# One of a band's sixteen transfers moves from SyncE's queue to GpSimd's

## The chip, the cores and the metric

The kernel runs on one core of a Trainium2 chip. The core has a matrix engine (TensorE, called PE in the profile), three engines for elementwise work (VectorE or DVE, ScalarE or ACT, GpSimd or POOL) and SyncE (SP), which here does nothing but issue DMA transfers. GpSimd issues transfers too. The transfers of both run on the same 16 DMA engines. Each engine works through its own list of instructions in order, and they wait for each other by semaphores. The metric is the time of one execution on the device in microseconds.

## What is computed

The input is `x`, 32 images of 256 channels and 32 x 32 pixels in float32. Two layers are added to it in turn:

```python
    # --- layer 0 (conv_preact) ---
    x = x + _L0_conv_ref(_gn(x), L0_conv_weight, L0_conv_bias)
    # --- layer 1 (conv_preact) ---
    x = x + _L1_conv_ref(_gn(x), L1_conv_w1, L1_conv_bn_gamma, L1_conv_bn_beta, L1_conv_bn_mean, L1_conv_bn_var, L1_conv_w2, L1_conv_b2)
```

`_gn` is a group norm with 32 groups. Layer 0 is a 3 x 3 convolution from 256 to 256 channels with its operands and its result rounded to a 16-bit float. Layer 1 is an involution: every pixel computes its own 7 x 7 filter for each of 16 groups of channels, and that filter is applied to the normalised input around the pixel:

```python
        y = jnp.einsum('oc,bchw->bohw', w1, x)
        ...
        w = jnp.einsum('oc,bchw->bohw', w2, y) + b2[None, :, None, None]
        w = w.reshape(b, G, K * K, H, W)
        ...
        out = jnp.einsum('bgkhw,bgckhw->bgchw', w, patches)
```

## The kernel before

An image passes through two halves that overlap with those of its neighbours. The front half (`front`) does the norm, the 3 x 3 convolution (line 332), the second norm and the transposed pixels (line 396). The back half is the involution, and it has a detour through memory in the middle.

`weights` (line 411, PE) computes the filters of four image rows at a time, and `evict` (line 435, DVE) adds their bias and lays them into the ring buffer `w_sb` in SBUF. `scatter` (line 476, SP) writes the filters of eight image rows into the scratch tensor `wd` in device memory, in seven transfers of 160 KB, so that each pixel's filter lands at a shifted place. `load_bands` (line 497) reads the same eight rows back as a band: a matrix that says how every source pixel of these rows contributes to the pixels in its 7 x 7 surroundings. `sums` (line 522, PE) multiplies pixels by the band in 128 small matmuls per band, and `add_windows` (line 538, DVE) adds the result into `x`. `store` (line 543, SP) writes the image out, and `load_x` (line 106, SP) brings in later images.

There are four bands to an image and so 128 in all. A band is read in 16 transfers, one for each value of `j`, which is a column of a half image. Most are of 70.5 KB; the three columns nearest the image's edge have part of their filter cut off and are shorter: `j` = 0 has 40.5 KB, `j` = 1 has 50.5 KB and `j` = 2 has 60.5 KB. The transfers are issued in the order of the list `ORDER`, and the list `BY_SYNC` names the values of `j` that SP issues:

```python
BY_SYNC = (0, 1)
ORDER = (0, 4, 8, 2, 12, 5, 9, 13, 3, 1, 6, 10, 14, 7, 11, 15)
...
            queue = nc.sync if j in BY_SYNC else nc.gpsimd
```

So POOL issues 14 of a band's 16 transfers and SP two. POOL does nothing else after the start. SP has the scatters, the images' loads and the stores between its band transfers.

The order of the work is written by hand. A loop counts steps `n`; an image takes 16 of them (`per`), a band four. `sums` of a band stands at its step, `weights` 18 steps ahead (`LEAD`), the scatters one and two steps behind the weights that complete them, and `load_bands` nine steps ahead of the use (`due(n, 3 - 4 * NBAND)`). There are three band buffers (`NBAND`). A band's transfers wait until PE has finished with the band three before it, and until the scatter of their rows has landed. The transfers of each queue take eight completion semaphores in turn. An issue on POOL waits for the landing of the transfer that was issued eight before it on POOL; SP has eight semaphores of its own.

Of the kernel before, what the change touches and what calls it, by code (L numbers as in the profile page):

```python
# [62 lines left out]
ROW = S * WPIX  # L63
WR = 4
NBAND = 3
BY_SYNC = (0, 1)
ORDER = (0, 4, 8, 2, 12, 5, 9, 13, 3, 1, 6, 10, 14, 7, 11, 15)
NPIX = 6
RING = 32
# [9 lines left out]
def tile_quant_conv_then_involution(  # L79
# [398 lines left out]
    def load_bands(b, k):  # L478
# [3 lines left out]
        for i, j in enumerate(ORDER):  # L482
# [12 lines left out]
            )  # L495
            queue = nc.sync if j in BY_SYNC else nc.gpsimd
            queue.dma_start(to, src)  # L497
# [140 lines left out]
```

## Time and profile before

| what | value |
|---|---|
| runs, median (lowest to highest) | 1353.61 us (1353.46 to 1360.37) |
| the profiled execution's own time | 1351.29 us |
| its span, first to last instruction | 1349.5 us |
| PE busy | 1247.6 us, 92% |
| POOL busy | 1012.5 us, 75% |
| DVE, ACT busy | 827.1 us, 734.2 us |
| moved by DMA | 361.85 MB, 268 GB/s over the span |
| band issues on POOL, line 497 | 1792, mean 550 ns, median 548 |
| band issues on SP, line 497 | 256, median 593 ns |

The profile is one execution. An issue of a transfer counts as busy time on POOL, but not on SP, whose issues appear only in the timeline and in the rows of a single line. A wait is put down to what ended last before the engine went on: "POOL band L497 <- DMA band<-wd" is time in which POOL stood before an issue of line 497 until a transfer from `wd` into a band had landed. "issue" as the cause means that the profile shows none. The three numbers of a wait are its total in us, how often it occurred, and the longest. A row of a group gives busy time, mean ns of one instruction, and the idle time of the engine just before them with what ended most of it. The chain that ended last is followed back from the last instruction, at each step to what released it.

### The profile page before, as it was taken

To read this page: it belongs to the slowest core of one execution; us is meant where nothing else is said; L and a number is where in the kernel's file an instruction comes from. 1 tells how busy PE (TensorE), PEld (TensorE's weight loads), DVE (VectorE), ACT (ScalarE), POOL (GpSimd) and SP (SyncE) were. 2 spreads that over 40 slices of the span, in tenths; PEclk is the share of its full clock that TensorE was granted. 3 is DMA by queue.
4 is the path that set the end of the run, shared out by engine and by line. 5 is a ranking of instruction groups with operands and counts; after the bars stand their busy time and mean duration, and the time that the engine had idled before them with its cause. 6 is when DMAs were issued, how large, how long until landed. Compare 5 with 4: busy or idle time off the path is not lost.

```text
span 1349.5 us, 65799 instructions
## 1 busy us (share of the span) xinstructions
PE 1247.6 (92%) x27648; PEld 757.6 (56%) x27648; DVE 827.1 (61%) x2539; ACT 734.2 (54%) x1731; POOL 1012.5 (75%) x1818
## 2 busy tenths in 40 slices
PE   4899999999989999999999999999999999999664
PEld 2355556655545665555566556555655556555453
DVE  5456656666656666666666566666666566566542
ACT  5875655555646556565555556555656565563300
POOL 9067777787778778877778777777877877788885
PEclk9999999999999999999999999999999999999997
DMA  6089999999999999999999999999999999999995
GB/s 227 6 236 295 270 271 284 283 278 296 282 271 286 297 287 281 298 282 281 267 285 287 260 282 282 271 284 284 288 285 278 274 280 278 277 285 262 282 270 157
DMA packets 360724, 361.85 MB, mean 268 GB/s; under 512 B 75056, under 2 KB 304752, under 8 KB 359152
## 3 DMA queue, kind: packets, MB, share of 16 engines
q1 hardware_dynamic: 278512, 229.38, 56.5%
q0 software_dynamic: 81920, 128.28, 33.5%
q8 instruction: 220, 3.60, 1.1%
q14 instruction: 72, 0.59, 0.1%
HBM read 176.60 MB, written 180.76 MB: 265 GB/s over the span
## 4 chain that ended last, share of the span: by engine, by line
PE 58%; DMA 24%; POOL 8%; issue 4%; DVE 3%; ACT 2%; SPq 1%; POOLq 0%; DVEq 0%; ACTq 0%
PE pc L332 24%; DMA band<-wd 19%; PE acc L522 18%; PE pw L411 10%; POOL band L497 8%; DMA wd<-w_sb 4%; PE py L377 3%; PE pt L396 3%; ACT junk L214 1%; DVE w_sb L435 1%; SPq L476 1%; DVE wq L195 1%; DVE x L538 1%; DMA band<-in_w 1%; DMA out<-x 0%
## 5 line engine op out<-in xcount | busy, mean ns | idle before, releaser
L497 POOL DMA_DIRECT2D band<-wd x1792 | 980.8, 550 | 320.5 <-DMA band<-wd 189.9
L435 DVE TENSOR_TENSOR w_sb<-pw,late_sb 128x224 f32<-128x224 f32 (+7 forms) x1280 | 331.4, 324 | 423.6 <-PE pw L411 423.4
L332 PE MATMUL pc<-xq,wq 128*128 128x496 f16 (+3 forms) x2304 | 535.1, 378 | 25.0 <-ACT xq L273 20.6
L522 PE MATMUL acc<-band,pixels 64*32 64x190 f32 (+1 forms) x16384 | 423.5, 330 | 55.5 <-DMA band<-wd 44.2
L522 PEld LDWEIGHTS acc<-band,pixels 64*32 64x32 f32 x16384 | 301.6, 107 | 164.7 <-issue 88.9
L332 PEld LDWEIGHTS <-wq 128*128 128x128 f16 x2304 | 206.3, 98 | 322.9 <-issue 106.7
L411 PE MATMUL pw<-late_sb,y 64*32 64x224 f32 (+1 forms) x8192 | 285.0, 330 | 14.1 <-issue 12.7
L538 DVE TENSOR_TENSOR x<-acc,x 128x380 f32<-128x380 f32 (+1 forms) x512 | 262.4, 513 | 35.5 <-PE acc L522 26.6
L411 PEld LDWEIGHTS pw<-late_sb,y 64*32 64x32 f32 x8192 | 183.7, 105 | 38.7 <-issue 22.3
L400 ACT COPY pixels<-pt 128x512 f32<-128x512 f32 x128 | 73.8, 577 | 226.5 <-PE pt L396 226.5
L214 ACT ACTIVATE junk<-x 128x512 f16<-128x512 f32 (+1 forms) x192 | 146.4, 762 | 11.9 <-DVE x L348 9.4
L214 ACT ACTIVATE junk<-x,mean 128x1024 f16<-128x1024 f32 x128 | 147.1, 1149 | 4.3
L245 ACT ACTIVATE s<-back,eps 128x2 f32<-128x2 f32 x64 | 18.9, 296 | 178.8 <-DVE back L230 178.8
L273 ACT ACTIVATE xn<-x,off,rstd 128x512 f32<-128x512 f32 x128 | 96.1, 800 | 0.0
L346 DVE TENSOR_SCALAR q<-pc 128x512 f16<-128x512 f32 x128 | 87.2, 681 | 13.3 <-PE pc L332 13.3
L348 DVE SCALAR_TENSOR_TENSOR x<-q,early_sb,x 128x512 f32<-128x512 f16 x128 | 94.7, 740 | 0.3
L396 PE MATMUL pt<-ident,xn 128*128 128x128 f32 x512 | 77.8, 275 | 1.5 <-ACT pixels L400 1.4
L396 PEld LDWEIGHTS pt<-ident,xn 128*128 128x128 f32 x512 | 63.7, 142 | 27.3 <-issue 2.8
L273 ACT ACTIVATE xq<-x,off,rstd 128x1024 f16<-128x1024 f32 x64 | 75.6, 1227 | 0.0
L235 ACT ACTIVATE mean<-back 128x2 f32<-128x2 f32 x64 | 12.6, 196 | 100.0 <-DVE back L230 100.0
L377 PE MATMUL py<-xn,early_sb 128*64 128x512 f32 x256 | 62.2, 605 | 0.9 <-ACT xn L273 0.9
L388 ACT ACTIVATE y<-py,bn_shift,bn_scale 128x256 f32<-128x256 f32 x64 | 32.5, 557 | 23.3 <-PE py L377 23.0
(40 smaller groups left out, 368.2 us busy)
## 6 DMA issues: line engine op xcount, KB each, us to landing
wd<-w_sb SPq DMA_DIRECT2D x896, 160.0 KB
band<-wd POOLq DMA_DIRECT2D x1664, 70.5 KB
x<-in_x SPq DMA_DIRECT2D x64, 512.0 KB
out<-x SPq DMA_DIRECT2D x64, 512.0 KB
band<-wd POOLq DMA_DIRECT2D x128, 60.5 KB
band<-wd SPq DMA_DIRECT2D x128, 50.5 KB
band<-wd SPq DMA_DIRECT2D x128, 40.5 KB
band<-in_w SPq DMA_DIRECT2D x2, 1152.0 KB
```

The lines of the kernel that those rows point to most:

```text
L214: nc.scalar.activation(junk[:, n0:n1], src[:, h, n0:n1], func, bias=bias, accum_out=self.sums[:, i : i + 1])
L273: nc.scalar.activation(dst, src, AF.Identity, bias=self.off[:, one], scale=self.rstd[:, one])
L332: nc.tensor.matmul(pc.rearrange("p (r c) -> p r c", c=W)[:, r0 - nt * RT : r1 - nt * RT, c0:c1], wq[:, kh, k, mh * P : (mh + 1) * P], xq[: ...
L346: nc.vector.tensor_scalar(q, pc, F16_MAX, -F16_MAX, ALU.min, ALU.max)
L348: nc.vector.scalar_tensor_tensor(xt[:, mh, cols], q, bias_sb[:, mh : mh + 1], xt[:, mh, cols], ALU.add, ALU.add)
L377: nc.tensor.matmul(py[i * CR : (i + 1) * CR], w1_sb[:, kh, :], px[:, :, i], start=kh == 0, stop=kh == CH - 1,)
L396: nc.tensor.transpose(pt[:, i, h * P : (h + 1) * P], xn[:, h, (m + i) * P : (m + i + 1) * P], ident)
L411: nc.tensor.matmul(pws[i][t * TW : (t + 1) * TW, : dj.stop - dj.start, r], y_sb[b % 2][half, (r0 // 2 + r) * W : (r0 // 2 + r + 1) * W], w ...
L435: nc.vector.tensor_tensor(to, of[:, :, d0:d1], bias[:, :, d0:d1], ALU.add)
L497: queue.dma_start(to, src)
L522: nc.tensor.matmul(at[t * TW : (t + 1) * TW, h, :, f - top : l - top], px[p, a, v * GC : v * GC + TW], of[:, :, a, f - top : l - top, v], ...
L538: nc.vector.tensor_tensor(x_at, of, x_at, ALU.add)
```

## The change

The transfer with `j` = 1 is issued by GpSimd in place of SyncE. SP keeps `j` = 0 alone, and POOL issues 15 transfers for each band. In POOL's list the transfer comes ninth of fifteen, as `ORDER` says.

```diff
--- before.py
+++ after.py
@@ -63,7 +63,7 @@
 ROW = S * WPIX
 WR = 4
 NBAND = 3
-BY_SYNC = (0, 1)
+BY_SYNC = (0,)
 ORDER = (0, 4, 8, 2, 12, 5, 9, 13, 3, 1, 6, 10, 14, 7, 11, 15)
 NPIX = 6
 RING = 32
```

## The prediction

> **What bounds the kernel now.** I read the page's table of engines first, then the chain that ended last, then the waits of PE and of POOL, then POOL's row among the groups, and last the stretches of POOL alone.
>
> ```profile
> PE 1247.6 (92%) x27648; PEld 757.6 (56%) x27648; DVE 827.1 (61%) x2539; ACT 734.2 (54%) x1731; POOL 1012.5 (75%) x1818
> ...
> PE 58%; DMA 24%; POOL 8%; issue 4%; DVE 3%; ACT 2%; SPq 1%; POOLq 0%; DVEq 0%; ACTq 0%
> ```
>
> By busy time PE is the bound. The chain gives PE 58%, but a third of the span (DMA 24%, POOL 8%) runs over the band loads and the engine that issues them, so PE is not alone.
>
> ```profile
> L497 POOL DMA_DIRECT2D band<-wd x1792 | 980.8, 550 | 320.5 <-DMA band<-wd 189.9
> ```
>
> This is GpSimd's whole steady work: 1792 issues (128 bands of 14), 550 ns each. The reader is to see that its 75% is not idle for want of a task; the waits, POOL's and one of PE's, say what fills the rest:
>
> ```profile
> POOL band L497 <- DMA band<-wd: 189.9, 246, 3.6
> ...
> POOL band L497 <- DMA wd<-w_sb: 62.8, 27, 38.2
> POOL band L497 <- issue: 52.9, 61, 3.7
> PE acc L522 <- DMA band<-wd: 44.2, 19, 5.9
> ...
> POOL band L497 <- PE pt L396: 5.7, 4, 2.0
> ...
> POOL band L497 <- PE acc L522: 0.7, 3, 0.4
> ```
>
> A band's first issue has to wait until PE has freed the band buffer. POOL loses only 0.7 us to that in the whole run: the buffer has always been free for a while when POOL comes to it. So POOL is never ahead. What it waits for is its own earlier transfers (189.9 us, 246 times): in the order of instructions with their semaphores POOL's transfers take eight completion semaphores in turn, and each issue waits for the landing of the one eight before it. I call this the lane wait. 38.2 us of the 62.8 us on `wd` is a single wait, at the start. PE in turn waits 44.2 us for bands. POOL's stream of issues and PE run at nearly the same pace, and POOL is the one that is behind.
>
> The pace in stretches of POOL's issues (us, then busy and count, granted clock, DMA share, GB/s):
>
> ```profile
> 400.00:600.00 200.00, 156.90 (x288) 1.00 0.98 289
> ...
> 800.00:1000.00 200.00, 154.47 (x283) 1.00 0.96 283
> 1000.00:1200.00 200.00, 151.37 (x277) 0.99 0.95 278
> 1200.00:1250.00 50.00, 41.31 (x77) 1.00 0.94 273
> ```
>
> An issue comes every 0.69 to 0.72 us, and every 0.65 us once the last images have been loaded. The DMA engines are 94 to 98% busy, so bytes are close to a limit too. POOL's first issue starts at 73.1 us, its last ends at 1336.2 us (the row of line 497): 1263.1 us for 1792, 0.705 us each. 13.3 us remain to the end of the span.
>
> **The time that the sum is made against.** The profiled execution took 1351.3 us, span 1349.5 and 1.8 around it. The median of the runs is 2.3 us higher, which is added at the end.
>
> **The change, part by part.** In each of 128 bands the transfer with j = 1 (50.5 KB) leaves SP's queue for POOL's. PE, DVE and ACT keep their order; bytes, buffers and the shape of the transfer stay.
>
> SP loses 128 of 256 band issues. Their row has a median of 593 ns, so some 76 us of issue time go. I cost this at nothing: SP's queue has 1% of the chain, and it has waits of its own on DVE (150.7 us for `w_sb`) to fall back on. What was queued behind the moved issue, the scatters, can be issued 0.6 us earlier per band, which bears on POOL's wait for `wd` below.
>
> POOL gains 128 issues: 128 x 0.550 = +70.4 us. In the new order the issue stands ninth of fifteen, behind the transfer j = 3, and six further issues of its band are queued behind it. PE waits for the last of these. Nothing hides this: POOL waits for no other engine long enough, and cover would have to come out of its own waits. They are, term by term:
>
> - Lane waits. Now 189.9 / 1792 = 0.106 us per transfer. If that pace holds, 128 more transfers cost 128 x 0.106 = +13.6 us. From the other side: between 1200 and 1250 us, without image loads, the wait is 6.0 us for 77 transfers, 0.078 each; 1920 x 0.078 = 149.8, or -40.1 us. A longer run spreads the same bytes and lightens the DMA engines (283 GB/s now in the middle, a few per cent less then), which shortens landings; but a band's image loads and stores stay. I take the middle, -13.2 us.
> - Waits of no shown cause (52.9 us): 61 of them, spread over the stream, so by count, 52.9 x 128 / 1792 = +3.8 us.
> - Waits for `wd`: 62.8 - 38.2 = 24.6 us can go, as POOL comes later to each band and SP's scatters are issued earlier; or nothing goes, as a slower POOL also holds back PE, DVE and the scatters. Half: -12.3 us.
> - Waits for PE (pt 5.7, acc 0.7, pw 0.7 us): too small to count.
>
> Sum: 70.4 - 13.2 + 3.8 - 12.3 = +48.7 us, or 1400 us on the profiled execution and 1402 us on the median (3.6% up). All of it reaches the end, because POOL's last band is followed only by the 13.3 us tail. As a pace: (1263.1 + 48.7) / 1920 = 0.683 us per transfer. Ends: low 70.4 - 40.1 + 3.8 - 24.6 = +9.5, 1363 us; high 70.4 + 13.6 + 3.8 = +87.8, 1441 us, which is the present pace times fifteen.
>
> A rule weighed against the rows. The two queues' issue costs are 548 ns median for POOL and 593 for SP in the rows of line 497, so the move makes no single issue dearer. The Trainium skill, "DMA: Bandwidth & Descriptors", section "SWDGE vs HWDGE vs iDMA", sends plain copies to SP or ACT because their setup is faster. That speaks against the move but for a reason that this row does not show. The same page, section "Issuing engines are not separate DMA queues", says that spreading issues over engines saves only the time to initiate, usually small beside the transfer. By it the move would be worth almost nothing and the time would stay at 1354. The trace's answer is that initiating is not small here: 981 us of POOL's 1263.
>
> **The rivals.**
>
> A. Hidden: no change, 1351 to 1354 us on the median. PE is 92% busy and waits for bands 44.2 us in only 19 waits; three band buffers could soak up a later POOL. For no change the pace must reach 1263.1 / 1920 = 0.658 us per transfer, which only the 1200 to 1250 stretch beats (0.649). Against it: a stock of ready bands would show as POOL waiting for a free buffer, and that is 0.7 us.
>
> B. The pace does not improve at all, or gets worse: 1441 us and above. For it: the stretches from 400 to 1200 us differ by only 4% in pace whatever the DMA share. Against: the image-free stretch, and a DMA load that must fall as the run grows.
>
> C. Faster, by one mechanism: SP's queue, lighter by one transfer per band, leaves the DMA engines to POOL's transfers, these land before their lane is wanted again, and the lane waits collapse. It decides below the pace of 0.658. The other gaps after the change are (52.9 + 3.8 + 62.8 + 7.1) / 1920 = 0.066 us, so with the 0.550 of an issue the lane wait would have to fall below 0.042 from 0.106. At 0.028 the time would be 1920 x 0.014 = 27 us less, 1327 us. It is bounded by PE's 44.2 us of band waits: not below 1309. Against: the DMA engines move the same bytes, and the lowest lane wait in a stretch is 0.078.
>
> D. That SP's part of a band is what PE waits for, so that the move takes it off the late queue. PE's chain enters bands through POOL's issues (8%) and not SP's (1%, its scatters). If it were so, up to the 44.2 us of PE's waits would be at stake, less what POOL adds. I give it no chance of its own; it is in C.
>
> **How the numbers follow.** The forecast (pace 0.668 to 0.700, 1373 to 1434 us) 0.73; B with its approaches (over 1434) 0.11; a cheap outcome, 1361 to 1373, 0.05; A, within 0.5% (1347 to 1360; 0.5% is about what a measurement here can tell from no change), 0.07; C 0.04. The range runs from the low end of the sum, 1363, to its high end, 1440: about 0.14 lies below and 0.05 above. Faster 0.04, same 0.07, slower 0.89.
>
> **What would show it.** In the profile after: POOL's row at line 497 x1920, still near 550 ns, some 1056 us busy; POOL's share of the span at 78%; POOL's wait for its own bands between 150 and 204 us; still no wait of POOL for acc; PE's wait for bands well above 44 us and PE's share near 89%; the chain moved from PE to DMA and POOL; DMA moving near 258 GB/s over the span. I am wrong if an issue on POOL lasts longer, if lane waits fall below 0.05 us per transfer (A or C), or if PE's band waits don't grow.

## The result, and the profile after

The change makes the kernel slower: median 1427.15 us (1422.48 to 1429.03) against 1353.53 us, a ratio of 1.056 (95% interval 1.0527 to 1.0593), some 74 us. The prediction said 1402 us, between 1363 and 1440.

The profiled execution after took 1427.95 us, 76.7 us more than that of before. Its engines and the chain that ended last, from the page:

```profile
span 1426.2 us, 65827 instructions
...
PE 1275.1 (89%) x27648; PEld 775.9 (54%) x27648; DVE 819.1 (57%) x2539; ACT 736.0 (52%) x1731; POOL 1085.7 (76%) x1946
...
PE 45%; DMA 32%; POOL 8%; issue 5%; DVE 4%; SPq 3%; ACT 3%; POOLq 0%; DVEq 0%; ACTq 0%
```

PE's share of the chain falls from 58% to 45% and DMA's rises from 24% to 32%. PE is busy for 89% of the span, not 92%. The cost stands in POOL's row, and the waits tell how it is made up (total us, times, longest):

```profile
L497 POOL DMA_DIRECT2D band<-wd x1920 | 1051.6, 550 | 326.7 <-DMA band<-wd 194.9
```

```profile
POOL band L497 <- DMA band<-wd: 194.9, 231, 2.8
...
PE acc L522 <- DMA band<-wd: 80.6, 41, 4.9
POOL band L497 <- issue: 57.7, 79, 3.0
POOL band L497 <- DMA wd<-w_sb: 54.5, 35, 36.3
```

The row adds up to the whole rise. Busy time goes from 980.8 to 1051.6 us (+70.8), the idle time before the issues from 320.5 to 326.7 (+6.2): together +77.0, where the span grew by 76.7. That the sum comes out is no proof by itself, since POOL's list runs in both kernels from shortly after the start (first issue at 73.1 and 71.0 us) to 13 us before the end. What the row shows is which part grew: 128 more issues at an unchanged 550 ns took 71 us, and POOL's waits together got no shorter to make room for them (those for `wd` fell from 62.8 to 54.5 us, the others grew by more). PE's wait for bands went from 44.2 to 80.6 us.

The time that SP gained turned into waiting. Its largest waits after (SP's own queue, same columns):

```profile
SPq L476 <- DVE w_sb L435: 355.0, 98, 47.6
SPq L106 <- DMA out<-x: 115.2, 27, 6.3
```

Its wait for the filters in `w_sb` was 150.7 us before and is 355.0 us now: SP stands in front of its scatters until DVE has written the filters. About half of that rise is SP's own freed time, since the same wait is 260.5 us in a kernel below in which SP has one band transfer and the run is as quick as before. That the rest comes from PE waiting longer for bands is argued from the order of the work, not shown.

### The profile page after: what moved, and what is told of

Its sections match the earlier page's. It is cut to its first block, busy times and chain, and to the rows that moved or that the text cites. A ratio compares the mean times of both kernels' runs of the same rounds, so it can differ in the third digit from the quotient of the medians.

```text
span 1426.2 us, 65827 instructions
## 1 busy us (share of the span) xinstructions
PE 1275.1 (89%) x27648; PEld 775.9 (54%) x27648; DVE 819.1 (57%) x2539; ACT 736.0 (52%) x1731; POOL 1085.7 (76%) x1946
## 2 busy tenths in 40 slices
DMA packets 361748, 361.87 MB, mean 254 GB/s; under 512 B 77104, under 2 KB 306800, under 8 KB 360176
## 4 chain that ended last, share of the span: by engine, by line
PE 45%; DMA 32%; POOL 8%; issue 5%; DVE 4%; SPq 3%; ACT 3%; POOLq 0%; DVEq 0%; ACTq 0%
DMA band<-wd 24%; PE pc L332 17%; PE acc L522 15%; PE pw L411 9%; POOL band L497 8%; DMA wd<-w_sb 7%; SPq L476 3%; PE py L377 3%; DVE w_sb L435 2%; PE pt L396 1%; ACT junk L214 1%; DVE x L538 1%; DMA band<-in_w 1%; ACT xn L273 0%; DVE x L348 0%
## 5 line engine op out<-in xcount | busy, mean ns | idle before, releaser
L497 POOL DMA_DIRECT2D band<-wd x1920 | 1051.6, 550 | 326.7 <-DMA band<-wd 194.9
L522 PE MATMUL acc<-band,pixels 64*32 64x190 f32 (+1 forms) x16384 | 438.7, 336 | 102.2 <-DMA band<-wd 80.6
L522 PEld LDWEIGHTS acc<-band,pixels 64*32 64x32 f32 x16384 | 312.3, 108 | 216.3 <-issue 119.1
L411 PE MATMUL pw<-late_sb,y 64*32 64x224 f32 (+1 forms) x8192 | 294.4, 336 | 20.2 <-issue 18.7
L411 PEld LDWEIGHTS pw<-late_sb,y 64*32 64x32 f32 x8192 | 191.0, 107 | 47.2 <-issue 30.5
## 6 DMA issues: line engine op xcount, KB each, us to landing
band<-wd POOLq DMA_DIRECT2D x128, 60.5 KB, 3.9
band<-wd POOLq DMA_DIRECT2D x128, 50.5 KB, 4.9
```

What stands on the lines that cost most here:

```text
L411: nc.tensor.matmul(pws[i][t * TW : (t + 1) * TW, : dj.stop - dj.start, r], y_sb[b % 2][half, (r0 // 2 + r) * W : (r0 // 2 + r + 1) * W], w ...
L522: nc.tensor.matmul(at[t * TW : (t + 1) * TW, h, :, f - top : l - top], px[p, a, v * GC : v * GC + TW], of[:, :, a, f - top : l - top, v], ...
```

## The experiments

Theory: the time is set by POOL's list of issues; one more issue per band costs its 0.55 us and the list's usual waits, whatever it carries. I call it the stream theory. Rivals were that the 50.5 KB on another queue cost the time, that SP's lighter list does, and that PE or the DMA engines bind so that POOL's list matters little. Ratios are against the kernel before, run beside each group of experiments on the same chip.

### One more issue that carries almost nothing

```diff
             queue.dma_start(to, src)
+            if j == 1: nc.gpsimd.dma_start(spare, bass.AP(tensor=src.tensor, offset=src.offset, ap=[src.ap[0], src.ap[1], [1, PAD]]))
```

This is put into the kernel before, with a small tile `spare`.

> SP keeps its two transfers of a band; POOL issues a fifteenth per band, right behind j = 3, that reads 8 floats for each of 16 rows (512 bytes) into a spare tile. Nothing of the result depends on it. Stream theory (the time is set by POOL's list of issues, and an issue costs 0.55 us and its share of the waits whatever it carries): 1415 to 1430 us, as with the moved transfer, POOL's row x1920. Rival (the cost is that 50.5 KB more go through POOL's queue, and landings get later for it): the small one costs little, below 1380 us. Rival (what SP no longer issues makes the rise, through an order that suited less): 1354 us.

Measured: 1421.9 us, ratio 1.0475 (1.0415 to 1.0534). The added issue's line (its duration in ns, lowest, median and highest, and the first and last start) with the time from issue to landing in us, and the two waits:

```profile
L498 POOL DMA_DIRECT2D spare<-wd x128: 567/567/570, 75.4 to 1403.4; - x128
...
DMA to landing us min/median/max: 2.2/5.1/7.8
```

```profile
POOL band L497 <- DMA band<-wd: 167.6, 201, 2.8
...
PE acc L522 <- DMA band<-wd: 68.6, 39, 5.7
```

A transfer of 512 bytes that nobody reads costs 0.0475 x 1357.65 = 64 us, or 0.50 us per issue; the moved 50.5 KB cost 0.056 x 1353.53 = 76 us, 0.59 each. So most of the cost is the place in POOL's list. The difference of about 11 us is for bytes and landings, if it is real: the two intervals just overlap. The added issue also takes its turn among the eight semaphores, so its 0.567 us on POOL and its turn are not told apart here.

### The moved transfer issued by nobody

```diff
-        for i, j in enumerate(ORDER):
+        for i, j in enumerate(j for j in ORDER if j != 1):
```

> The transfer j = 1 is issued by nobody; POOL has 14 and SP one. The part of the result that comes from these columns is left out. It is the change without POOL's part. Stream theory: POOL's list is that of the kernel before, so 1345 to 1355 us; at most some 20 us less if 3% fewer bytes shorten landings (lane waits 189.9 to 170). Rival (an SP that is lighter lets its scatters burst against POOL's transfers): above 1375 us.

Measured: 1355.8 us, ratio 1.001 (0.9976 to 1.0044). Taking the issue from SP is worth nothing that can be told from zero, even with its bytes gone too (355.22 MB moved for 361.85). POOL's wait for its own transfers was not less, and SP's wait for the filters grew:

```profile
POOL band L497 <- DMA band<-wd: 200.6, 247, 2.8
```

```profile
SPq L476 <- DVE w_sb L435: 260.5, 92, 48.0
```

The two halves of the change thus stand apart: SP's half is near 0, and POOL's half is 64 us for the issue alone and about 76 us with the bytes.

### Sixteen and thirteen on POOL

```diff
-BY_SYNC = (0, 1)
+BY_SYNC = ()          # e16
+BY_SYNC = (0, 1, 2)   # e13
```

> SP issues none of a band's transfers, POOL all 16. Stream theory: the pace after was (1413.0 - 71.0) / 1920 = 0.699 us for each; at 2048 the time is 2048 x 0.699 + 85 + 2 = 1518 us, or 90 us over the changed kernel; with nothing but the issue's own 0.55 us it is 70 us over, 1497 us. Rival (DMA engines get free as the run grows, and landings get shorter): below 1475 us. Lane waits near 190 us in total if only the issue is added, 207 us if they go with the count.

> SP issues j = 0, 1 and 2, POOL 13. Stream theory: 1664 x 0.70 = 1165 us for POOL's list alone, 1252 us in all, so POOL is no longer what ends last; PE is, with its 44 us of waits for bands and little else to lose: 1305 to 1330 us. Rival (DMA engines were 95% busy and bind as much as POOL does): 1340 to 1355 us. Rival (SP's own list, with 128 more issues of 0.6 us, delays the scatters): above 1360 us, with POOL's wait for wd well over 60 us.

Sixteen: 1505.9 us, ratio 1.109 (1.1018 to 1.1162), 0.109 x 1357.65 / 256 = 0.58 us for each of 256 added issues. It lies between the two prices of the stream theory, 1497 and 1518 us. The lane waits went up:

```profile
POOL band L497 <- DMA band<-wd: 214.8, 239, 3.2
```

That is near the 207 us of waits that go with the count, though from 14 to 15 issues they had risen by only 5.0 us. The step from 14 to 15 and the step from 15 to 16 cost about the same. The landings should have been the place where a longer run pays back. The middle of the run from 200 to 1200 us, line 497 on POOL alone (busy and count, granted clock, DMA share, GB/s), of the kernel before, of the changed one and of the one with sixteen:

```profile
200.00:1200.00 1000.00, 769.79 (x1407) 1.00 0.96 282
```

```profile
200.00:1200.00 1000.00, 777.76 (x1422) 0.98 0.91 264
```

```profile
200.00:1200.00 1000.00, 779.57 (x1424) 0.96 0.88 249
```

The DMA share falls from 0.96 to 0.91 to 0.88, and POOL makes 1407, 1422 and 1424 issues in the same millisecond. Its pace is 0.70 to 0.71 us per issue with 14, 15 or 16 to a band. The time from issue to landing (the last number) fits that, first after, then with sixteen:

```profile
band<-wd POOLq DMA_DIRECT2D x1664, 70.5 KB, 4.5
```

```profile
band<-wd POOLq DMA_DIRECT2D x1664, 70.5 KB, 4.5
band<-wd POOLq DMA_DIRECT2D x128, 60.5 KB, 4.0
band<-wd POOLq DMA_DIRECT2D x128, 50.5 KB, 4.9
```

The median is 4.5 us at both DMA shares. For the kernel before, the page gives no landing time; the landing events in its trace, matched to the issues by semaphore, give about 4.6 us. So landings got some 2% quicker while the share fell by five points. It is not a matter of the transfer's own size either: 50.5 KB take longer than 60.5, and the 512 bytes of the first experiment took 5.1 us.

Thirteen: 1376.0 us, ratio 1.0139 (1.0077 to 1.0201), slower than fourteen. The stream theory's 1305 to 1330 us is wrong here; the time and the waits are those that the rival of SP's list gave. POOL's waits:

```profile
POOL band L497 <- DMA wd<-w_sb: 174.2, 75, 36.7
POOL band L497 <- DMA band<-wd: 164.0, 218, 3.1
```

The wait for `wd` rises from 62.8 to 174.2 us: POOL stands before the first transfer of a band in place of a later one. That SP's scatters come too late because three band issues stand among them is one reading; that a POOL with fewer issues simply comes earlier to each band is another, and the last experiments bear on it.

### What makes the landings

Both start from the changed kernel.

```diff
-            n = (K1 - cut) * WB + PAD
+            n = min(K1 - cut, 3) * WB + PAD                    # short15
...
-                ap=[[WPIX, TW], [ROW, TR], [1, WB]],
+                ap=[[WPIX, TW], [ROW, TR], [1, WB // 2]],      # scat15, and the same cut of the rows in w_sb
```

> The changed kernel with every band transfer cut to at most 3 of its 7 filter columns: the same 1920 issues on POOL, 8 rows by 2 sides each, with 1952 bytes for 4512 per row; the left-out columns of the bands stay zero, so that part of the result is missing. Theory A (landings follow the bytes that POOL itself has in flight): the lane waits go from 194.9 us to under 60, and the time to 1290 to 1340 us, where PE ends last. Theory B (landings are set by a fixed delay and by SP's transfers on the same DMA engines): lane waits stay above 140 us and the time above 1385 us.

> The changed kernel with SP's scatters halved: rows of 320 bytes in place of 640, the same number of rows and of issues; the scratch tensor is filled with zeros once at the start, which adds some 5 MB there. Half of every filter is left out of the result. Theory B with SP's bytes as the cause: lane waits under 100 us and 1310 to 1350 us. Theory A, or a delay by count of rows and not bytes: lane waits 150 to 195 us, 1385 to 1430 us.

Measured: short15 1325.4 us, ratio 0.9754 (0.9698 to 0.981), though POOL still issues 1920 times; scat15 1359.4 us, ratio 1.003 (0.9994 to 1.0066). Rows of POOL and its waits, short15 and then scat15:

```profile
L497 POOL DMA_DIRECT2D band<-wd x1920 | 1063.2, 557 | 215.4 <-DMA band<-wd 101.5
```

```profile
L497 POOL DMA_DIRECT2D band<-wd x1920 | 1054.4, 552 | 248.8 <-DMA band<-wd 147.4
```

Neither theory fits alone. The lane waits fall from 194.9 to 101.5 us when most of POOL's own transfers shrink to less than half, and to 147.4 us when SP's scatters are halved. The bytes saved are about the same (285.85 and 293.91 MB moved for 361.87), and the landing median of POOL's transfers is 3.9 us in both. So bytes of both queues delay the landings, and by the waits, not by the median landing, POOL's own weigh more. That agrees with the rest: POOL always has up to eight transfers under way, and neither the change nor the sixteen alters what these eight and SP's burst of scatters carry while they are in flight. They alter only the quiet time between. This last step is argued, not shown. It also puts a limit on the stream theory: the count of issues alone does not set the time. In short15 the 1920 issues still keep POOL busy for 1063.2 us, but its idle time falls by 111 us, and a list of 15 is then quicker than the kernel before with 14. PE has 82% of the chain that ended last there.

### The transfer on a third engine

ScalarE can issue transfers too. In act14 SP has one, ACT one (`j` = 1) and POOL 14; in act13 SP has two, ACT one (`j` = 2) and POOL 13.

```diff
-            queue = nc.sync if j in BY_SYNC else nc.gpsimd
+            queue = nc.sync if j in BY_SYNC else nc.scalar if j == 1 else nc.gpsimd   # act14, BY_SYNC = (0,)
+            queue = nc.sync if j in BY_SYNC else nc.scalar if j == 2 else nc.gpsimd   # act13
```

> SP issues j = 0, ScalarE's queue j = 1, POOL 14. SP is as light as in the change, POOL's list as in the kernel before. Stream theory: no rise, 1340 to 1360 us, unless ACT is held up before its issue. Rival (the rise comes from SP's lighter list or from the order in which the transfers land): above 1400 us.

> SP issues j = 0 and 1, ScalarE's queue j = 2, POOL 13. With SP's list as before, POOL's 13 should not wait for wd more than before (62.8 us; 174.2 us with three on SP). Stream theory: POOL's list is 1664 x 0.70 = 1165 us and PE ends last: 1305 to 1335 us, which beats both kernels. Rival (the DMA engines bind at 95% share): 1345 to 1357 us. Rival (ACT, held up by an issue that waits for its band buffer, delays the norms): above 1360 us.

Measured: act14 1410.3 us, ratio 1.0402 (1.0325 to 1.0479); act13 1445.4 us, ratio 1.0649 (1.0578 to 1.072). By the expectation for act14 this speaks for the rival, but its waits name another cause. ACT's, in act14:

```profile
ACT pixels L400 <- DMA wd<-w_sb: 124.3, 21, 7.7
...
ACT xq L273 <- DMA wd<-w_sb: 93.4, 27, 4.6
```

ACT works its list in order, and its issue of a band transfer waits until the scatter has landed. The norms and pixels queued behind it wait as well, 218 us in these two rows; neither occurs in the kernel before. There POOL lost only 24.6 us to scatters after its first issue. In act14 its waits for `wd` are 133.8 us, so its list did not stay as it was either, and act14 can't decide between the theory and the rival.

So the issue on ACT was put three steps later, in a second call of `load_bands` for ACT's values of `j` alone, which the first call then leaves out:

```diff
+            b, i = due(n, 3 + 3 - 4 * NBAND)
+            if b is not None and i % 4 == 0:
+                load_bands(b, i // 4, True)
```

> SP issues j = 0, ACT j = 1 three steps later, POOL 14: the changed kernel with the moved transfer taken off POOL's list, and a whole result. Stream theory: as the kernel without j = 1, 1345 to 1362 us. Rival (POOL's list isn't the cause of the rise): 1400 us or more.

> As the version with SP 2, ACT 1 and POOL 13, but ACT's issue of j = 2 stands three steps (some 7.5 us) later in the program than the band's other transfers, when the scatter has mostly landed. Stream theory: ACT's waits for wd go from 286 us in two rows to under 60, SP's waits for band landings from 112 us to under 30, and POOL's list of 13 no longer ends last: 1310 to 1345 us. Rival (an issue costs ACT 0.6 us in a place where the norms are on the path, or SP's list binds as it did with three on SP): 1355 to 1400 us.

> SP issues j = 0, ACT j = 1 and j = 2 three steps later, POOL 13. SP's and POOL's lists are both shorter than in the kernel before, ACT's longer by 256 issues. Stream theory: 1300 to 1335 us with PE ending last; POOL's waits for wd no higher than 70 us. Rival (ACT's path): above 1355 us.

Measured: act14_late3 1364.1 us, ratio 1.0046 (1.0023 to 1.0069). SP is as light as in the change, all 16 transfers are made, POOL has 14, and the rise of 5.6% is down to 0.5%; the 1364.1 us are 2 us above the expected range. act13_late3 1352.8 us, ratio 0.9944 (0.9908 to 0.998), between the ranges of the theory and the rival. act13_sp1_late3 1349.3 us, ratio 0.9929 (0.9896 to 0.9962): the quickest of the versions that compute everything, 0.7% under the kernel before, and far from the 1300 to 1335 us expected. The middle of the run (PE, PEld, DVE, ACT, POOL, then clock, DMA share, GB/s), first of the kernel before, then of that version, and that version's longest waits of POOL and one of SP:

```profile
200.00:1200.00 1000.00, 966.73 (x21773) 589.08 (x21768) 637.28 (x1989) 572.88 (x1355) 769.79 (x1407) 1.00 0.96 282
```

```profile
200.00:1200.00 1000.00, 964.71 (x21700) 589.03 (x21696) 633.46 (x1975) 577.36 (x1352) 715.03 (x1304) 1.00 0.97 280
```

```profile
POOL band L497 <- DMA band<-wd: 188.5, 230, 3.5
POOL band L497 <- DMA wd<-w_sb: 139.2, 56, 37.1
```

```profile
SPq L476 <- DMA band<-wd: 73.7, 49, 4.8
```

POOL is busy for 715 us of 1000, but the DMA share is 0.97 and PE is busy for 965 us, as it was in the kernel before (967 us at 0.96). By these shares PE and the DMA engines were already close to their limits with fourteen issues on POOL, which would leave a shorter list little to gain; no run tests this. The lane waits do not shrink with the list (188.5 us for 1664 issues).

POOL now waits for scatters, and a lighter SP does not cure it: with 13 on POOL the wait for `wd` is 174.2 us when SP has three band transfers, 133.7 when it has two and 139.2 when it has one (the others late on ACT). So SP's third issue alone does not explain the rise from 62.8 us. But the late issues on ACT bring a wait of their own: SP stands before its scatters for 73.7 us (44.6 in act13_late3, 2.5 in the kernel before) until band transfers have landed. What makes POOL wait for `wd` with 13 thus stays open. That three on SP are worse than two with one on ACT is shown by the times, 1.0139 against 0.9944.

## Why the prediction was right, and where its size was off

The direction and the mechanism were right: POOL's list sets the pace, 128 issues of 0.550 us are added to it, nothing covers them, and SP's share costs and gains nothing that can be told from zero (the kernel without `j` = 1 stands at 1.001; with the transfer on ACT, late enough, at 1.0046). Measured 1427 lies in the range but 25 us over the forecast. The terms of its sum, by the two profiled executions:

| term | forecast, us | measured, us |
|---|---|---|
| issues | +70.4 | +70.8 (980.8 to 1051.6) |
| lane waits | -13.2 | +5.0 (189.9 to 194.9) |
| waits of no shown cause | +3.8 | +4.8 (52.9 to 57.7) |
| waits for `wd` | -12.3 | -8.3 (62.8 to 54.5) |
| other idle time in the row | 0 | +4.7 (14.9 to 19.6) |
| sum | +48.7 | +77.0 |

The step that failed in size is the lane waits, 18 of the 28 us. The prediction took the middle between the present pace and the pace of the 50 us stretch without image loads, because a longer run "lightens the DMA engines" and "shortens landings". The share did fall, from 0.96 to 0.91 in the middle of the run, and the landings hardly followed: medians of about 4.6 us before and 4.5 us at 0.91 and 0.88, and 1407, 1422 and 1424 issues per millisecond. The quick stretch had no image loads on SP, and its own DMA share was 0.94, so a mean share is not what made it quick. The changed kernel has the same stretch behind its last image load, at 1237 us, with the same 77 issues in 50 us at a share of 0.86 (line 497 on POOL alone):

```profile
1250.00:1300.00 50.00, 41.92 (x77) 0.97 0.86 245
```

So the quick pace comes back at quite different shares. The 3 x 3 convolutions of line 332 still run in both stretches (81 and 90 of their matmuls), so they are not what is missing; that the missing loads make the pace is argued, since no run leaves them out. As short15 and scat15 show, landings get shorter when transfers in flight get smaller. The high end of the sum, where the present wait per issue holds, was the better estimate.

On the rivals. A, hidden, falls with the first experiment: an issue that carries almost nothing costs 64 us, so there is no stock of bands to cover it. B, no better pace at all, has the right idea, and its 1441 us are 14 us high: the pace went from 0.705 to (1413.0 - 71.0) / 1920 = 0.699 us. C, lane waits that collapse with a lighter SP, falls with the kernel without `j` = 1: they were 200.6 us there. Its threshold also has a slip: the 62.8 us of waits for `wd` include the 38.2 us ahead of POOL's first issue, which are no part of the 1263.1 us, so the lane wait would have had to fall below 0.062 us and not 0.042; measured were 194.9 / 1920 = 0.102. D, that PE waits for SP's part of a band, falls with the result itself, since PE's waits for bands grew when that part became smaller.

Of the signs named in the prediction, most came: 1051.6 us busy for 1056, lane waits of 194.9 within 150 to 204, 0.8 us of waiting for a free buffer, PE's wait for bands at 80.6 us, PE at 89%, 254 GB/s for 258. Two did not: POOL's share is 76% and not 78%, since the span is longer than forecast, and the chain moved from PE to DMA only, with POOL's own share of it still at 8%.

The page of the Trainium skill, "DMA: Bandwidth & Descriptors", says under "Issuing engines are not separate DMA queues" that the time to initiate a transfer is usually small beside the transfer. For a single transfer the trace agrees: 0.55 us of issue beside 4.5 us to landing. But here the landings overlap and the issues of one engine do not, so the small part decided: 0.50 us of run time for each added issue of 512 bytes.

## What to carry to other kernels

Before moving a transfer between queues, look at the list of each issuing engine for what it waits for: a list that waits mostly for its own earlier transfers, and hardly ever for a free buffer, can set the pace even at 75% busy, and here nearly every issue added to it was paid in full. Price such an issue at the list's present pace, waits included, and don't count on landings getting quicker because the run gets longer. Don't turn the sum round either: here an issue taken off the list gained next to nothing, probably because other limits stood close by. An issue put on an engine that computes must stand late enough in its list that what it waits for has already happened.

## What was not expected

- A shorter list on POOL gained nothing by moving the issue to SP: thirteen are slower than fourteen (1.0139), with 174.2 us of waits for scatters. Neither direction is free.
- Where an issue stands in ACT's list is worth more than the issue: act14 went from 1.0402 to 1.0046, and act13 from 1.0649 to 0.9944, by three steps of the loop.
- The mean clock granted to TensorE fell as PE idled more: 0.985 before, 0.971 after, 0.948 with sixteen on POOL (PE busy for 92%, 89% and 86% of the span), and the busy time of the same 27648 matmuls rose from 1247.6 to 1275.1 and 1295.0 us. POOL's waits for PE were 7 us before and 9 us after, and in the middle of the run PE was busy for 925 us of 1000 after the change and 967 before, so a slower PE is not needed to explain the rise.
